# Five instead of six of twelve multiplications by C on GpSimd, in the scan of a hybrid vision kernel

## The chip, the cores and the metric

The kernel runs on one core of one Trainium2 chip. A core has TensorE (PE, matrix products; its weight loads are listed apart as PEld), VectorE (DVE), ScalarE (ACT), GpSimd (POOL) and SyncE (SP, which here issues the DMA transfers). Each engine works through its own instructions in the order in which they were issued to it, and waits for others through semaphores. The metric is the device time of one execution in microseconds; lower is better. Three runs of the kernel before took 6701.09 to 6705.06 us, median 6704.47.

## What is computed

The input is a batch of four images of 96 channels and 64 x 64 pixels. Four layers follow each other; only the first matters here. It normalises the image, expands it to 192 channels, applies a 3 x 3 depthwise convolution and SiLU, and then runs a selective scan over the 4096 pixels in four directions (K = 4: rows, columns, and both reversed), with 16 states for each channel:

```
def step(hst, inp):
    ut, dt_, bt, ct = inp
    dA = jnp.exp(dt_[..., None] * A[None])
    hst = hst * dA + (dt_ * ut)[..., None] * bt[:, :, None, :]
    y = jnp.einsum('bkdn,bkn->bkd', hst, ct)
    return (hst, y)
h0 = jnp.zeros((b, K, DI, N), jnp.float32)
_, ys = jax.lax.scan(step, h0, (u_t, d_t, B_t, C_t))
```

So for each state: a decay exp(delta x A), an input delta x u x B, the recurrence h = h x decay + input, the product h x C, and a sum of these products over the 16 states. The other layers are an inverted residual convolution block, a Fourier attention with a feed-forward block in rounded numbers, and a linear attention with such a block.

## The kernel before

**Tiling of the scan.** A step is one image, one direction and one chunk of 512 pixels: 4 x 4 x 8 = 128 steps. The 192 x 16 states of a step are cut into 12 units (`PC`, numbered u = 0 to 11), each of two halves (e = 0, 1) of 128 partitions by 512 pixels, where the 128 partitions are 32 channels by 4 states. That makes 1536 units. The order of the units within a step is two channel blocks for each of four groups of states (u = 0 to 7), then the third channel block for the four groups (u = 8 to 11).

**What a unit does.**
- `inputs` (L1206): GpSimd multiplies delta x u by B for both halves at once (128 x 1024), into `db`, which has three buffers.
- `decays` (L1216): ScalarE takes two exponentials into two PSUM banks `ps_da`. Four banks have that tag, so two units are there at a time.
- `states` (L1225): VectorE runs the recurrence, one instruction for each half. Its start value comes from the state that the unit of the same number left in the step before.
- The product with C, on one of two engines. In a GpSimd unit the scan writes to an SBUF tile `hc` (five buffers), and `product` (L1244) multiplies both halves in place with one GpSimd instruction. In a VectorE unit the scan writes back over its own PSUM bank, and VectorE multiplies each half right behind its scan from there into `hc` (L1229).
- `keep`: the last column of the states is put by for the next step: by two small copies on ScalarE in a VectorE unit (L1239), by one on GpSimd in a GpSimd unit (L1241). In the last chunk of a direction nothing is kept.
- `sums` (L1265): TensorE adds up over the states, four matmuls for each unit into a bank `ps_y`, for pairs of units (0 and 1, 2 and 3, and so on). At the end of each pass ScalarE takes the bank out (L1276), and SyncE stores it.

Which engine multiplies is fixed by one list, `POOL_C` at L45, read where the units are made (L1169, `"pool": u in POOL_C`). The functions that ask for it are these:

```
x["h"] = [x["hc"][:, e] for e in (0, 1)] if x["pool"] else x["da"]
...
                if not x["pool"]:
                    x["made"] = nc.vector.tensor_mul(x["hc"][:, e], x["h"][e], x["step"]["BC"][x["j"]][:, 1])
...
                if not x["pool"]:
                    nc.scalar.copy(to[:, e : e + 1], x["h"][e][:, end : end + 1])
                elif e == 0:
                    nc.gpsimd.tensor_copy(to, x["hc"][:, :, end])
```

**The order on the engines.** The scan is written under a manual schedule: the order of the program is the order on each engine. A turn of the loop (a slot) deals with one unit and its neighbours: transfers due for the next step and stores (SyncE); `keep` for unit slot - 1 and `decays` for unit slot + 1; `product` for unit slot - 1, if it is a GpSimd unit; `inputs` for unit slot + 2; `states` for unit slot; and the sums of a pair two turns after its second unit.

**The work beside the scan.** The convolutions, norms and the other layers of the neighbouring images fill the same engines. They are written as generators in stages ("front", "turn", "conv", "spectral", "layer_2", "layer_3"). At the end of each turn, `advance` takes steps from them as long as a budget of work for this turn (`owed`, `rate`) and a room for each engine (`room`, `SHARE`) allow it, by prices in microseconds that are written beside each step. None of these asks for `POOL_C`. Operations that appear in the text are, in the front stage, the three ScalarE steps of softplus (L603 to L607), VectorE's L609 and L612 behind them, and ScalarE's copy L616, which gives the bank back; and VectorE's L872 in the layer norms. After the last unit, from about 6210 us, the rest of the last image runs alone.

Of the kernel before, what the change touches and what calls it, by code (L numbers as in the profile page):

```python
# [41 lines left out]
KORDER = [(0, 1, 3, 2)] * (B - 1) + [(1, 3, 0, 2)]  # L42

SCAN = {"rep_d": 3, "rep_g": 3, "rep_BC": 5, "db": 3, "hc": 5}
POOL_C = (1, 3, 5, 7, 9, 11)  # L45
TMP, IN = 10, 5

PC = NI * NJ // 2
# [46 lines left out]
def hybrid_kernel(ctx: ExitStack, tc: tile.TileContext, a: dict):  # L95
# [1052 lines left out]
    def scans(stages):  # L1148
# [13 lines left out]
        for number, step in enumerate(steps):  # L1162
            step["at"] = number % (K * NCH)
            u = 0
            for which, chans in enumerate(PASSES):
                for j in range(NJ):
                    for i in chans:
                        units.append({"step": step, "number": number, "u": u, "j": j, "i": i, "pass": which,
                                      "pool": u in POOL_C})  # L1169
                        u += 1  # L1170
# [402 lines left out]
```

## Time and profile before

| | us |
|---|---|
| median of three runs | 6704.47 |
| the profiled execution | 6709.47 |
| span of its instructions | 6707.7 |
| VectorE busy, 60 to 6210 us | 5304.58 |
| GpSimd busy, 60 to 6210 us | 5480.56 |
| ScalarE busy, 60 to 6210 us | 3990.90 |
| TensorE busy, 60 to 6210 us | 4405.08 |

The profile is of one execution. A row of its costliest groups has the line, the engine, the operation, output and inputs by name, their shapes and the number of instructions; then the busy time in us and the mean in ns; then the idle time of the engine just before these instructions with what ended most of it. Busy time counts each moment of an engine once, so that overlapping instructions add up to less than number times mean. A line of busy time in a stretch gives the stretch, its length, the busy time of each engine with the number of instructions, the granted clock of TensorE (1 is full), the share of the DMA engines and GB/s. A line of waits gives the waiting engine, its output and line, what it waited for, then the sum in us, how often, and the longest. The scan runs from about 70 to 6210 us of the span. GpSimd has almost nothing but the scan: L1206, L1244 and L1241.

### The profile page before, as it was taken

The numbers are of one execution on the slowest core, as the hardware profiler recorded it, in microseconds if no ns is written. First come the engines' busy times: TensorE is split into PE (matmuls) and PEld (weight loads), VectorE is DVE, ScalarE is ACT, GpSimd is POOL, SyncE is SP. The second block draws the span as 40 slices with busy tenths as digits, with TensorE's granted clock in tenths as the row PEclk, the third lists the DMA queues.
The fourth block names the chain that finished last, engine by engine and source line by source line (L and its number), as shares of the span: only waits on it lengthen the run. The fifth ranks groups of instructions, "written<-read, shape, count | busy, mean of one in ns | idle before, by whom it ended". The sixth has DMA issues, their size and how long they took to land. (4 is left out here: it accounts for less than half of the span.)

```text
span 6707.7 us, 84354 instructions
## 1 busy us (share of the span) xinstructions
PE 4872.1 (73%) x27884; PEld 1775.4 (26%) x27884; DVE 5391.2 (80%) x5611; ACT 4269.2 (64%) x8008; POOL 5488.7 (82%) x2983
## 2 busy tenths in 40 slices
PE   7624767656987776775688877777887776859998
PEld 2101212111223521221122254211223521212383
DVE  5979888788989888888899887988988888888021
ACT  5744776654665677877466657866665676756356
POOL 4868778788999999977999988999999899899000
PEclk9756878768998887886799877878998877869998
DMA  5644555566544544455764445465644554554131
GB/s 189 197 150 144 183 189 181 174 218 219 184 148 143 199 158 147 155 186 188 246 214 146 143 160 167 157 219 186 188 147 146 189 161 161 200 180 156 35 94 38
DMA packets 438824, 1121.41 MB, mean 167 GB/s; under 512 B 73002, under 2 KB 74768, under 8 KB 437140
## 3 DMA queue, kind: packets, MB, share of 16 engines
q1 hardware_dynamic: 438388, 1116.02, 50.7%
q8 instruction: 222, 3.64, 0.2%
q14 instruction: 214, 1.75, 0.1%
HBM read 881.28 MB, written 239.01 MB: 167 GB/s over the span
## 5 line engine op out<-in xcount | busy, mean ns | idle before, releaser
L1206 POOL TENSOR_TENSOR db<-rep_g,rep_BC 128x1024 f32<-128x1024 f32 x1536 | 3602.0, 2365 | 194.1 <-DVE ps_da L1225 115.0
L1216 ACT ACTIVATE ps_da<-rep_d,aneg 128x512 f32<-128x512 f32 x3072 | 2053.5, 689 | 499.4 <-DVE hc L1225 381.7
L1225 DVE TENSOR_TENSOR_SCAN ps_da<-ps_da,state,db 128x512 f32<-128x512 f32 x1344 | 1722.9, 1282 | 371.8 <-ACT state L1239 226.7
L1244 POOL TENSOR_TENSOR hc<-hc,rep_BC 128x1024 f32<-128x1024 f32 x768 | 1813.4, 2361 | 131.8 <-DVE hc L1225 64.8
L1225 DVE TENSOR_TENSOR_SCAN hc<-ps_da,state,db 128x512 f32<-128x512 f32 x1344 | 1645.8, 1266 | 173.0 <-ACT ps_da L1216 155.9
L1265 PE MATMUL ps_y<-hc,cst 128*32 128x512 f32 x6144 | 1037.4, 755 | 781.5 <-POOL hc L1244 759.5
L1229 DVE TENSOR_TENSOR hc<-ps_da,rep_BC 128x512 f32<-128x512 f32 x1536 | 1062.3, 692 | 91.3 <-DVE ps_da L1225 1.3
L1265 PEld LDWEIGHTS ps_y<-hc,cst 128*32 128x32 f32 x6144 | 141.7, 119 | 1450.8 <-POOL hc L1244 1096.0
L1241 POOL COPY state<-hc 128x2 f32<-128x2 f32 x672 | 128.4, 191 | 395.3 <-DVE hc L1225 374.1
L1239 ACT COPY state<-ps_da 128x1 f32<-128x1 f32 x1344 | 212.8, 158 | 343.9 <-DVE hc L1229 343.0
L805 PE MATMUL ps_mm<-h,wd 128*32 128x512 f32 x3192 | 365.7, 593 | 7.7 <-ACT r L154 7.0
L543 PE MATMUL ps_mm<-xp,taps 128*128 128x512 f32 x576 | 299.3, 660 | 42.5 <-ACT xp L523 15.7
L1276 ACT COPY yt<-ps_y 128x512 f32<-128x512 f32 x256 | 149.9, 585 | 222.3 <-PE ps_y L1265 212.2
L594 PE MATMUL ps_mm<-xd,dtw 128*128 128x512 f32 x256 | 176.9, 785 | 156.9 <-ACT z L616 131.9
L782 PE MATMUL ps_mm<-wd,w 128*32 128x512 f32 x2128 | 271.4, 624 | 22.9 <-DMA wd<-x 12.8
L1225 DVE TENSOR_TENSOR_SCAN ps_da<-ps_da,db 128x512 f32<-128x512 f32 x192 | 234.6, 1222 | 56.9 <-ACT state L1239 36.0
L1225 DVE TENSOR_TENSOR_SCAN hc<-ps_da,db 128x512 f32<-128x512 f32 x192 | 223.4, 1204 | 17.3 <-ACT ps_da L1216 13.2
L603 ACT ACTIVATE z<-ps_mm 128x512 f32<-128x512 f32 x192 | 114.3, 596 | 189.1 <-PE ps_mm L594 112.4
L609 DVE SCALAR_TENSOR_TENSOR ps_mm<-ps_mm,z 128x512 f32<-128x512 f32 x192 | 131.9, 687 | 84.0 <-ACT z L607 56.4
L864 PE MATMUL ps_mm<-r,cst 128*128 128x512 f32 x210 | 144.9, 778 | 62.7 <-ACT r L154 17.4
L940 PE MATMUL ps_mm<-wa,xp 128*64 128x96 f32 x1728 | 133.3, 317 | 71.0 <-DVE d L944 62.3
L786 ACT ACTIVATE h<-ps_mm 128x512 f32<-128x512 f32 x266 | 153.9, 596 | 44.6 <-PE ps_mm L782 42.5
(418 smaller groups left out, 6879.9 us busy)
## 6 DMA issues: line engine op xcount, KB each, us to landing
rep_BC<-bc SPq DMA_DIRECT2D x512, 512.0 KB
rep_g<-du SPq DMA_DIRECT2D x384, 512.0 KB
rep_d<-delta SPq DMA_DIRECT2D x384, 512.0 KB
y<-yt SPq DMA_DIRECT2D x512, 128.0 KB
du<-g SPq DMA_DIRECT2D x128, 256.0 KB
delta<-z SPq DMA_DIRECT2D x128, 256.0 KB
tab<-in_etab SPq DMA_DIRECT2D x128, 256.0 KB
ypart<-y SPq DMA_DIRECT2D x72, 256.0 KB
```

The costliest lines, as they stand in the source:

```text
L543: mm(p, lhsT=taps[:, t, 0:128], rhs=window(t, c + e), start=t == 0, stop=t == 8)
L594: mm(p, lhsT=dtw[:, o + 2 * part, 0:128], rhs=xd, start=True, stop=True)
L782: mm(p[32 * n : 32 * n + 32], lhsT=w1[:, 32 * g : 32 * g + 32], rhs=xin[:, n : n + 15 : 2, 1 : W + 1], start=True, stop=True)
L786: act(h[:, :, 1 : W + 1], split(p), AF.Relu)
L805: mm(p[32 * n : 32 * n + 32], lhsT=held["wd"][:, groups[i], o, dx, :], rhs=here[i][:, :, dx : dx + W], start=dx == 0, stop=dx == 2)
L1206: nc.gpsimd.tensor_mul(x["db"], x["step"]["g"][x["i"]], both(x["step"]["BC"][x["j"]][:, 0]))
L1216: act(x["da"][e], x["step"]["d"][x["i"]][:, e], AF.Exp, scale=aneg[:, av : av + 1])
L1225: nc.vector.tensor_tensor_scan(x["h"][e][:, order], x["da"][e][:, order], x["db"][:, e, order], start, ALU.mult, ALU.add)
L1229: x["made"] = nc.vector.tensor_mul(x["hc"][:, e], x["h"][e], x["step"]["BC"][x["j"]][:, 1])
L1239: nc.scalar.copy(to[:, e : e + 1], x["h"][e][:, end : end + 1])
L1244: x["made"] = nc.gpsimd.tensor_mul(x["hc"], x["hc"], both(x["step"]["BC"][x["j"]][:, 1]))
L1265: done = mm(y[32 * q : 32 * q + 32], lhsT=const("stack"), rhs=x["hc"][:, e], start=first or (x["pass"] == 0 and x["j"] == 0), stop=last or ...
```

## The change

One list is changed. In each step GpSimd multiplies by C in units 1, 3, 6, 8 and 10 instead of 1, 3, 5, 7, 9 and 11; units 0, 2, 4, 5, 7, 9 and 11 are VectorE units, where 0, 2, 4, 6, 8 and 10 were.

```diff
@@ -42,7 +42,7 @@
 SCAN = {"rep_d": 3, "rep_g": 3, "rep_BC": 5, "db": 3, "hc": 5}
-POOL_C = (1, 3, 5, 7, 9, 11)
+POOL_C = (1, 3, 6, 8, 10)
 TMP, IN = 10, 5
```

Over the 128 steps, 128 units go from GpSimd to VectorE. With a unit goes the place of its states (PSUM bank instead of `hc`) and the engine of its state copies.

## The prediction

> **What bounds the kernel now.** I read the busy shares of the page first, then the costliest groups, then busy time in stretches of the span, then the waits inside three of those stretches. The chain of waits I left aside: it begins at 6139 us, near the end of the scan, so it says nothing of the loop that is changed.
>
> ```profile
> PE 4872.1 (73%) x27884; PEld 1775.4 (26%) x27884; DVE 5391.2 (80%) x5611; ACT 4269.2 (64%) x8008; POOL 5488.7 (82%) x2983
> ...
> L1206 POOL TENSOR_TENSOR db<-rep_g,rep_BC 128x1024 f32<-128x1024 f32 x1536 | 3602.0, 2365 | 194.1 <-DVE ps_da L1225 115.0
> ...
> L1225 DVE TENSOR_TENSOR_SCAN ps_da<-ps_da,state,db 128x512 f32<-128x512 f32 x1344 | 1722.9, 1282 | 371.8 <-ACT state L1239 226.7
> L1244 POOL TENSOR_TENSOR hc<-hc,rep_BC 128x1024 f32<-128x1024 f32 x768 | 1813.4, 2361 | 131.8 <-DVE hc L1225 64.8
> L1225 DVE TENSOR_TENSOR_SCAN hc<-ps_da,state,db 128x512 f32<-128x512 f32 x1344 | 1645.8, 1266 | 173.0 <-ACT ps_da L1216 155.9
> ...
> L1229 DVE TENSOR_TENSOR hc<-ps_da,rep_BC 128x512 f32<-128x512 f32 x1536 | 1062.3, 692 | 91.3 <-DVE ps_da L1225 1.3
> ...
> L1241 POOL COPY state<-hc 128x2 f32<-128x2 f32 x672 | 128.4, 191 | 395.3 <-DVE hc L1225 374.1
> L1239 ACT COPY state<-ps_da 128x1 f32<-128x1 f32 x1344 | 212.8, 158 | 343.9 <-DVE hc L1229 343.0
> ```
>
> GpSimd (POOL) and VectorE (DVE) stand within two points of each other. The 1536 products for `db` are 12 units in each of 128 steps; the 768 products for `hc` are the six units that the change reduces. The other six are 1536 half-width products at L1229 on DVE. The last two rows are the state copies, two for a DVE unit on ScalarE (ACT), one for a GpSimd unit.
>
> The average hides three kinds of stretch:
>
> ```profile
> core 0: us, PE busy (x) PEld busy (x) DVE busy (x) ACT busy (x) POOL busy (x), PEclk, DMA share, GB/s
> 1660.00:2110.00 450.00, 379.34 (x2244) 107.31 (x2246) 408.88 (x416) 285.63 (x556) 444.98 (x244) 0.93 0.50 163
> 460.00:610.00 150.00, 35.61 (x148) 7.39 (x140) 147.38 (x163) 55.16 (x109) 115.26 (x57) 0.50 0.45 152
> 660.00:1410.00 750.00, 516.30 (x1526) 143.97 (x1522) 623.63 (x657) 525.10 (x968) 571.16 (x311) 0.79 0.56 181
> ```
>
> The first is POOL at 98.9%, the second DVE at 98.3%, in the third neither is full (DVE 83%, POOL 76%, ACT 70%). In the first, the waits of DVE in that window name its master, and POOL waits for no engine:
>
> ```profile
> DVE ps_da L1225 <- POOL db L1206: 29.3, 42, 1.1
> DVE ps_da L1225 <- ACT state L1239: 2.5, 3, 1.2
> ```
>
> In the third, ACT waits for a cool TensorE (granted clock 0.79), and DVE for ACT:
>
> ```profile
> ACT z L603 <- PE ps_mm L594: 62.7, 36, 5.1
> ACT z L603 <- PE ps_mm L598: 40.6, 26, 3.1
> ACT ub L556 <- PE ps_mm L552: 34.5, 8, 7.9
> ```
>
> I cut the scan from 60 to 6210 us into 123 slices of 50 us and took, for each, the busy time of each engine and of the `db` products; busy time of those products over 2.345 us (3602.0/1536) is the number of units, a twelfth of it the number of steps. With DVE at 47.5 us or more I call a slice DVE-bound, else with POOL at 47 or more POOL-bound:
> - POOL-bound: 58 slices, 66.8 steps of 43.4 us; mean DVE 44.6, POOL 49.1.
> - DVE-bound: 15 slices, 14.6 steps of 51.3 us; mean DVE 48.7, POOL 42.2.
> - neither: 50 slices, 46.6 steps of 53.6 us (DVE about 39.7, POOL about 40.0).
>
> **What the Trainium skill says.** "Trainium Kernel Development and Optimization", Key Constraints: GpSimd has no access to PSUM. That fits the two forms of L1225: a GpSimd unit scans into `hc`, a DVE unit into the PSUM bank `ps_da`. "GPSIMD Engine Reference", 3 Performance versus the Vector engine: a two-input elementwise operation is about twice as fast on VectorE. Here one unit costs 2361 ns on POOL and 2 x 692 = 1384 ns on DVE, a ratio of 1.7. The same page, 1 Specifications: both engines share SBUF interfaces, and DVE instructions with two SBUF inputs contend. L1229 reads one operand from PSUM, so more of it shouldn't slow POOL; the trace agrees so far as L1206 has a median of 2362 ns with L1229 running beside it. "Perfetto Trace Analysis", Identifying Performance Opportunities: the most contended engine can change between regimes, which is what the slices show.
>
> **The change part by part, for one step of 12 units.**
> - POOL loses one `hc` product, 2361 ns, and in 7 steps of 8 one state copy, 191 ns: 2361 + 167 = 2.53 us, 324 us over 128 steps.
> - DVE gains two products of 692 ns, and two scans that write PSUM instead of SBUF (1282 for 1266 in the rows, medians 1281 and 1260, so 2 x 0.021): 1.43 us, 183 us in all.
> - ACT gains two copies of 158 ns in 7 of 8 steps: 0.28 us, 35 us in all. Each is issued ahead of an exponential in ACT's order. Bounds: 0 where ACT waits for DVE anyway (343 us before L1239), 0.28 where it is the last to come.
> - The positions move from every odd unit to 1, 3, 6, 8, 10. DVE units now stand side by side at 4, 5 and at 11, 0. A DVE unit takes 2 x (1282 + 692) = 3.95 us, a GpSimd unit 2 x 1.27 = 2.53 us of DVE. POOL has 4.9 us of work where it follows a GpSimd unit and 2.35 elsewhere. Two DVE units in a row (7.9 us) against POOL's 7.2 or so for the same pair of turns let POOL run up to 1.6 us ahead; it can't go further than `db`'s three buffers. I looked for a loop that alternates between the engines and is longer than either alone: going from POOL to DVE leads to the unit two places on (a `db` is made for the unit after next), so each such alternation skips a unit of at least 2.35 us, and the most that it can pick up at a DVE pair is 3.95 - 2.35 = 1.6 us. So no mixed loop is longer, and the new order costs nothing as long as ACT is in time. Bounds: 0 to 0.7 us a step (one DVE product of a pair unhidden).
> - TensorE's sums: the same 4 matmuls a unit. For pair 4, 5 they no longer wait for POOL, and the GpSimd products of 6, 8, 10 come a turn earlier than those of 7, 9, 11 did. PE's 759.5 us of waiting before L1265 falls; I take nothing for it, since what it sets free is ACT's background, late only in the third kind of stretch (gain there 0 to 0.3 us a step).
> - No DMA, and no place of the background work in the queues, depends on the list: a turn of the loop is filled by fixed prices. SP's order is unchanged.
>
> **The sum by kind of stretch.**
> POOL-bound: in each slice I add 1.43 us a step to DVE, take 2.53 from POOL, keep the larger and divide by 0.989, the share that POOL itself reaches now. The 58 slices come to 2754 us instead of 2900: -146. The two loads have become almost equal (sums 2713 and 2708), so what is late next is DVE. In ten of the slices TensorE is 46 us busy or more of 50; holding each slice to its TensorE time gives 2767, -133. I take three quarters of this, since DVE isn't as even as POOL: its background comes in bunches and it has ACT upstream. -100 us, 1.5 us a step. Ends: -133 and -30.
> DVE-bound: 14.6 x 1.43 = +21 us; DVE's added work is bare here.
> Neither: DVE's 1.43 and ACT's 0.28 are 1.71 us a step, were all of it on the path. In the third window DVE idles 17% and it is ACT and TensorE that it waits for, but ACT's last copy of a front block (L616) in turn stands behind DVE's L609, which queues behind the scans. I take half, 0.85 x 46.6 = +40 us. Ends: 0 and +80.
> Sum: -100 + 21 + 40 = -39 us. The profiled execution took 6709.47 us (span 6707.7), 5.0 over the median of the runs, 6704.47. So 6670.5 for a run like the profiled one, and against the median 6665.
>
> **The rivals.**
> - The full gain (0.09): POOL-bound slices reach -133, and the DVE time added in the third kind hides behind ACT and TensorE (+15). -133 + 21 + 15 = -97: 6607. For: POOL waits on no engine in the first window. Against: DVE's bursts.
> - A draw (0.11): only half of -133 comes, and in the third kind a little over half of the 80 is paid: -66 + 21 + 45 = 0, so 6704.
> - Slower (0.36): DVE becomes the engine that everything queues behind. Place: DVE's in-order queue at L1225/L1229, with L609, L872 and the other background operations behind it; they give banks back to TensorE and inputs to ACT. Price: all of 1.71 us in 61.2 steps outside the POOL-bound slices, +105, and behind the pairs of DVE units ACT's exponentials come late, so that the POOL-bound steps keep only 0.5 us: -33. Sum +72: 6776. It decides from the point where the POOL-bound steps gain less than what the others pay: (21 + 40)/66.8 = 0.9 us a step with half the price, 1.6 with the whole. For: DVE waits 262.7 us for L1239 and 169 us for L1216 already. Against: in the POOL-bound window only 2.5 us of those.
> - That the change doesn't do what it says I give nothing: the flag alone chooses the branch in states, keep and product.
>
> **How the numbers follow.** Forecast 6665 with chance 0.44, its own range 6635 to 6690. Full gain 0.09, draw 0.11, slower 0.36. The range takes in the full gain and the lower half of the slower case: 6600 to 6760. This kernel's runs lie within 4 us of each other, so 0.2%, 13 us, is about what can be told from no change. Faster 0.53, within 0.2% 0.11, slower 0.36.
>
> **What would show it.** L1244 x640 at about 2360 ns, L1229 x1792 at 692, L1239 x1568, L1241 x560. From 1660 on the same work in about 432 us instead of 450, DVE near 98% and POOL near 95, and POOL waiting for DVE (L1225) where it waited for nothing. In 460 to 610 a stretch longer by about 4 us. DVE's busy time about 5574, POOL's about 5165. Wrong would be: DVE well under 95% in the conv stretches with waits for ACT, which would mean that the new order of units costs more than its work; or the front stretches (660 to 1410) longer by more than 23 us, that is the whole 1.71 us in each of its 13.3 steps (160 units).

## The result, and the profile after

The changed kernel takes 6710.65 us, median of 20 runs, against 6704.77 for the kernel before in 20 runs beside it. The ratio is 1.0011, 95% interval 1.0004 to 1.0018: slower by about a tenth of a per cent, inside the 0.2% that the prediction counted as no change. The forecast was 6665. The 20 runs of the kernel before spread over 22 us (6692.90 to 6715.30), where the prediction, from three, took 4.

The page of the changed kernel, busy shares and the groups that answer to those shown of before:

```profile
PE 4846.8 (72%) x27884; PEld 1770.8 (26%) x27884; DVE 5551.4 (83%) x5867; ACT 4312.1 (64%) x8232; POOL 5178.2 (77%) x2743
...
L1206 POOL TENSOR_TENSOR db<-rep_g,rep_BC 128x1024 f32<-128x1024 f32 x1536 | 3599.2, 2362 | 508.3 <-DVE ps_da L1225 412.6
...
L1225 DVE TENSOR_TENSOR_SCAN ps_da<-ps_da,state,db 128x512 f32<-128x512 f32 x1568 | 2006.6, 1280 | 280.4 <-ACT state L1239 216.1
L1244 POOL TENSOR_TENSOR hc<-hc,rep_BC 128x1024 f32<-128x1024 f32 x640 | 1509.7, 2359 | 136.7 <-DVE hc L1225 77.2
...
L1229 DVE TENSOR_TENSOR hc<-ps_da,rep_BC 128x512 f32<-128x512 f32 x1792 | 1239.3, 692 | 113.6 <-PE ps_y L1265 3.8
L1239 ACT COPY state<-ps_da 128x1 f32<-128x1 f32 x1568 | 247.7, 158 | 459.4 <-DVE hc L1229 456.0
...
L1241 POOL COPY state<-hc 128x2 f32<-128x2 f32 x560 | 105.0, 187 | 388.5 <-DVE hc L1225 358.5
```

The work moved as the diff says, to the instruction: 640 products on GpSimd at 2359 ns, 1792 on VectorE at 692 ns. GpSimd is busy 310 us less (5488.7 to 5178.2), VectorE 160 more. But GpSimd's idle time before L1206 rose from 194 to 508 us: what it was spared, it waits for VectorE's scans. With 256 more VectorE products in the run, the products of the two engines took as long as before (2362, 2359 and 692 ns), so the contention between them that the prediction looked for doesn't show.

The same three stretches of the span, after:

```profile
core 0: us, PE busy (x) PEld busy (x) DVE busy (x) ACT busy (x) POOL busy (x), PEclk, DMA share, GB/s
1660.00:2110.00 450.00, 388.95 (x2264) 111.39 (x2264) 437.08 (x454) 300.58 (x603) 438.92 (x236) 0.94 0.54 175
460.00:610.00 150.00, 33.88 (x138) 7.12 (x138) 147.31 (x155) 52.52 (x103) 101.23 (x50) 0.50 0.44 145
660.00:1410.00 750.00, 519.36 (x1553) 146.26 (x1552) 636.18 (x677) 522.36 (x982) 538.26 (x288) 0.80 0.55 179
```

In the first, the conv stretch, VectorE now reaches 97.1% and GpSimd still 97.5%: the two meet, as the sum expected. VectorE's waits in that window are almost gone; of the 29.3 us for GpSimd's `db` none is left (the view lists gaps of more than 0.15 us):

```profile
DVE ps_da L1225 <- ACT state L1239: 1.8, 3, 1.1
DVE ps_da L1225 <- ACT ps_da L1216: 0.8, 1, 0.8
DVE ps_mm L735 <- PE ps_mm L733: 0.8, 1, 0.8
```

So this stretch got faster, and something else was lost. To find it, both traces were cut at the first recurrence instruction of each of the 128 steps. Steps were put into classes by their busy shares before: GpSimd at 97% or more (57 steps: 37 in the conv stages and the last image's scan, 20 elsewhere), else VectorE at 95% or more (14), else mixed (57). Summed over the steps of each class, in us against the trace of before, with the experiments below beside it:

| class before | steps | the change | e1 | e2 | e10 | e6 | e13 |
|---|---|---|---|---|---|---|---|
| GpSimd full, conv | 37 | -48.1 | -68.5 | -0.5 | -62.8 | -50.4 | -2.6 |
| GpSimd full, elsewhere | 20 | +20.5 | +8.4 | +9.5 | +12.3 | +1.9 | +23.2 |
| VectorE full | 14 | +22.7 | -6.3 | +17.5 | +22.3 | -0.9 | +20.4 |
| mixed | 57 | +12.2 | -30.3 | +9.3 | -4.7 | -4.4 | +14.8 |
| all | 128 | +7.3 | -96.8 | +35.8 | -32.9 | -53.8 | +55.8 |

Each column is one profiled execution, so a few us in a class mean nothing: e5, which changes almost nothing, shows +6.1 in the second row and -6.7 in the fourth. The classes were picked in the trace of before, so steps that were short there by chance tend to come out longer elsewhere; in the 20 steps e6, which leaves them as they were, has +1.9. A few us of every entry in the second row, the change's +20.5 too, are no effect.

### The profile page after: what moved, and what is told of

It reads as the page before. It is cut to its first block, busy times and chain, and to the rows that moved or that the text cites. A ratio compares the mean times of both kernels' runs of the same rounds, so it can differ in the third digit from the quotient of the medians.

```text
span 6713.7 us, 84574 instructions
## 1 busy us (share of the span) xinstructions
PE 4846.8 (72%) x27884; PEld 1770.8 (26%) x27884; DVE 5551.4 (83%) x5867; ACT 4312.1 (64%) x8232; POOL 5178.2 (77%) x2743
## 5 line engine op out<-in xcount | busy, mean ns | idle before, releaser
L1206 POOL TENSOR_TENSOR db<-rep_g,rep_BC 128x1024 f32<-128x1024 f32 x1536 | 3599.2, 2362 | 508.3 <-DVE ps_da L1225 412.6
L1216 ACT ACTIVATE ps_da<-rep_d,aneg 128x512 f32<-128x512 f32 x3072 | 2065.8, 690 | 481.1 <-DVE hc L1225 337.4
L1225 DVE TENSOR_TENSOR_SCAN ps_da<-ps_da,state,db 128x512 f32<-128x512 f32 x1568 | 2006.6, 1280 | 280.4 <-ACT state L1239 216.1
L1244 POOL TENSOR_TENSOR hc<-hc,rep_BC 128x1024 f32<-128x1024 f32 x640 | 1509.7, 2359 | 136.7 <-DVE hc L1225 77.2
L1225 DVE TENSOR_TENSOR_SCAN hc<-ps_da,state,db 128x512 f32<-128x512 f32 x1120 | 1371.3, 1266 | 116.9 <-ACT ps_da L1216 81.2
L1265 PE MATMUL ps_y<-hc,cst 128*32 128x512 f32 x6144 | 1018.4, 741 | 584.3 <-DVE hc L1229 285.7
L1229 DVE TENSOR_TENSOR hc<-ps_da,rep_BC 128x512 f32<-128x512 f32 x1792 | 1239.3, 692 | 113.6 <-PE ps_y L1265 3.8
L1239 ACT COPY state<-ps_da 128x1 f32<-128x1 f32 x1568 | 247.7, 158 | 459.4 <-DVE hc L1229 456.0
L1241 POOL COPY state<-hc 128x2 f32<-128x2 f32 x560 | 105.0, 187 | 388.5 <-DVE hc L1225 358.5
L1225 DVE TENSOR_TENSOR_SCAN ps_da<-ps_da,db 128x512 f32<-128x512 f32 x224 | 273.3, 1220 | 43.7 <-ACT state L1239 40.2
L1225 DVE TENSOR_TENSOR_SCAN hc<-ps_da,db 128x512 f32<-128x512 f32 x160 | 186.1, 1204 | 15.2 <-ACT ps_da L1216 9.0
```

Source lines behind the costliest of these rows:

```text
L1206: nc.gpsimd.tensor_mul(x["db"], x["step"]["g"][x["i"]], both(x["step"]["BC"][x["j"]][:, 0]))
L1216: act(x["da"][e], x["step"]["d"][x["i"]][:, e], AF.Exp, scale=aneg[:, av : av + 1])
L1225: nc.vector.tensor_tensor_scan(x["h"][e][:, order], x["da"][e][:, order], x["db"][:, e, order], start, ALU.mult, ALU.add)
L1244: x["made"] = nc.gpsimd.tensor_mul(x["hc"], x["hc"], both(x["step"]["BC"][x["j"]][:, 1]))
L1265: done = mm(y[32 * q : 32 * q + 32], lhsT=const("stack"), rhs=x["hc"][:, e], start=first or (x["pass"] == 0 and x["j"] == 0), stop=last or ...
```

## The experiments

Times are medians; ratios are against runs of the kernel before on the same chip, with 95% intervals. The kernel before had medians between 6702.23 and 6703.65 there. Three theories were held against each other at first. A, the one of the forecast: a step whose GpSimd is full is paced by GpSimd. B: only the conv stage is; elsewhere a full GpSimd merely fills the time that the others need. C: the order of the units costs the time.

**e1: GpSimd's relief alone.**

```diff
-                if units[slot - 1]["pool"]:
+                if units[slot - 1]["pool"] and units[slot - 1]["u"] != 5:
```

> Six on GpSimd as before, but the product with C of unit 5 is left out in all 128 steps (so that unit reaches the sum without its C): POOL does 128 x 2.36 us less, VectorE nothing more. Theory A (what the prediction used: all steps with GpSimd near full are paced by GpSimd): the 57 steps with GpSimd at 97% or more go from 43.0 to about 40.8 us, -125 us in all, 6580. Theory B (only the conv stage is paced by GpSimd; in the attention and feed-forward stages the full GpSimd only fills the time that VectorE and ScalarE need): the 37 conv steps gain about 2.2 us each, -80, the 20 others nothing, 6625. Theory C (the order of the units costs the time): as A, since the order is kept.

6609.18 us, 0.9856 (0.9842 to 0.987), between A and B. The classes decide: conv -68.5, and the 20 other full steps +8.4 (e5: +6.1), though GpSimd had 2.36 us less to do in each. That is B. The 30 us that the mixed steps gain neither theory had; half of them (14.9) come from the ten mixed steps with GpSimd at 94 to 97%. A stretch outside conv shows B in one view: busy time from 2340 to 2780 us, of the kernel before, then of e1, then of the changed kernel.

```profile
2340.00:2780.00 440.00, 294.22 (x1256) 96.01 (x1249) 388.57 (x396) 351.36 (x672) 425.94 (x235) 0.78 0.46 152
```

```profile
2340.00:2780.00 440.00, 293.41 (x1008) 82.53 (x1007) 387.22 (x394) 347.95 (x673) 401.85 (x223) 0.77 0.46 150
```

```profile
2340.00:2780.00 440.00, 295.55 (x1397) 102.41 (x1394) 395.33 (x412) 351.96 (x679) 397.92 (x213) 0.79 0.46 153
```

The fifth busy time is GpSimd's: 96.8% before, 91.3% in e1. VectorE's, the third, stays at 388 and 387: as much of its work was done in the same 440 us, so the pace didn't follow GpSimd. In the kernel before this window is steps 44 to 53. Cut by steps, these ten took 440.9 us before, 447.4 in e1, and 447.4 in e5 and 443.8 in e6, whose products there are those of before: 23.6 us less of GpSimd work bought nothing. Whom VectorE waited for there was to be read before the change too; its longest waits in that window, kernel before:

```profile
DVE ps_da L1225 <- ACT state L1239: 19.4, 20, 2.4
DVE hc L1225 <- ACT ps_da L1216: 8.2, 11, 1.5
DVE ps_da L1225 <- POOL db L1206: 7.0, 10, 0.9
```

ScalarE 27.6 us, GpSimd 7.0. In e1 the same two lines for ScalarE stand at 23.0 and 10.1 us. In the conv stretch it had been GpSimd 29.3 and ScalarE 2.5. GpSimd is nearly as full here (96.8%) as there (98.9%); the releaser of VectorE's waits is another.

**e2: VectorE's load alone.**

```diff
                     x["made"] = nc.vector.tensor_mul(x["hc"][:, e], x["h"][e], x["step"]["BC"][x["j"]][:, 1])
+                elif u == 5:
+                    nc.vector.tensor_mul(x["da"][e], x["da"][e], x["step"]["BC"][x["j"]][:, 1])
```

> Six on GpSimd as before, and two extra VectorE products of 128 x 512 behind the scans of unit 5, in place in their PSUM banks, which nothing reads: VectorE does 128 x 1.4 us more, GpSimd nothing less. Theory A: +20 us in the 14 steps that VectorE bounds, up to +40 in the 57 mixed ones, 0 in the 57 full ones: about 6750. Theory B: the same +20, +10 to +20 in the mixed ones, 0 in the conv steps and +1 us in each of the 20 full steps outside conv: about 6755, told from A by those 20 steps. Theory C: as A.

6742.46 us, 1.0054 (1.004 to 1.0068). In conv the added work is free (-0.5, GpSimd covers it), in the steps that VectorE fills it is bare (+17.5), in the mixed ones it costs a ninth of the forecast's price for all of it (9.3 of 57 x 1.43 = 82). The 20 steps have +9.5, half of what B said. So in those 20 neither engine's work alone sets the pace; what does, no run singles out. The two halves add up to -53 us, but the change has +6. They can't simply add in conv, since each alone is measured beside an engine that has slack; e16 below measures how little that is, 11 us.

**e3 and e4: the same amounts in other orders.** e3 is five on GpSimd, 1, 3, 5, 7, 9; e4 is six, 2, 3, 5, 8, 9, 11.

```diff
-POOL_C = (1, 3, 5, 7, 9, 11)
+POOL_C = (1, 3, 5, 7, 9)
```

> Five on GpSimd, units 1, 3, 5, 7, 9: the same amounts as the change, but three VectorE units in a row (10, 11, 0). Theories A and B (amounts decide): within 10 us of the changed kernel, 6700 to 6720. Theory C (runs of VectorE units cost time, because ScalarE's exponentials or POOL's db come out of step): slower than the changed kernel by 20 us or more, 6730 and over.

> Six on GpSimd in another order, units 2, 3, 5, 8, 9, 11: the amounts of the kernel before, with two pairs of VectorE units and two of GpSimd units side by side. Theories A and B: within 10 us of the kernel before. Theory C: slower by 20 us or more, with waits for ACT before the scans.

e3: 6713.22 us, 1.0016 (1.0009 to 1.0023), like the changed kernel, against C. e4: 6757.49 us, 1.0076 (1.0062 to 1.009), against A and B: with six, order can cost 55 us. e4 has two GpSimd units side by side, which no five of this study has.

**e9 and e10: the change's amounts, spread evenly in the old order.**

```diff
+                elif e == 1:
+                    nc.vector.tensor_mul(x["da"][1][:, :66], x["da"][1][:, :66], x["step"]["BC"][x["j"]][:, 1, :66])
...
-            x["made"] = nc.gpsimd.tensor_mul(x["hc"], x["hc"], both(x["step"]["BC"][x["j"]][:, 1]))
+            n = CH - 99
+            x["made"] = nc.gpsimd.tensor_mul(x["hc"][:, :, :n], x["hc"][:, :, :n], x["step"]["BC"][x["j"]][:, 1:2, :n].to_broadcast([128, 2, n]))
```

> Units and order as before (six on GpSimd at 1, 3, 5, 7, 9, 11), but the change's amounts of work spread evenly: each GpSimd product covers 2 x 426 of 2 x 512 columns (the last 86 of each half go to the sum without C), about 0.39 us less, and each such unit has one extra VectorE product of 128 x 172 in place in its PSUM bank, about 0.25 us, which nothing reads. No state copy moves. If the amounts alone decide (GpSimd's relief and VectorE's load meet in each step, the order is free): like the change, 6700 to 6715. If the order of the units or the copies cost the rest: the sum of the two halves measured before, -93 + 40 = -53, so about 6650.

> As e9_spread, with the widths set by what it measured (346 ns for 172 columns, 692 for 512, so about 240 for 66; GpSimd 2.1 ns a column): VectorE gets 6 products of 128 x 66 a step, about 1.43 us, GpSimd's products cover 2 x 413 columns, about 2.5 us a step less; 99 columns of each half go to the sum without C. These are the change's amounts in the order of before. If the order of the units costs what is missing: 6650 to 6670. If the amounts meeting in each step do: 6695 to 6715.

e9 (widths 172 and 86) took 6706.9 us, 1.0009 (1.0001 to 1.0017), but missed its aim: a VectorE product of 172 columns took 346 ns and not 250, 2.07 us a step in place of 1.43. e10 (the widths above: 234 ns, 1.40 us a step) has the change's amounts: 6672.05 us, 0.995 (0.9938 to 0.9963). The amounts alone make the kernel faster by 31 us. The 38 us up to the changed kernel come with what else the list changes. The pieces and the shortened GpSimd products, e9 first, then e10:

```profile
L1247 POOL TENSOR_TENSOR hc<-hc,rep_BC 128x852 f32<-128x852 f32 x768 | 1533.1, 1996 | 128.5 <-DVE hc L1225 95.2
...
L1231 DVE TENSOR_TENSOR ps_da<-ps_da,rep_BC 128x172 f32<-128x172 f32 x768 | 265.5, 346 | 26.6
```

```profile
L1247 POOL TENSOR_TENSOR hc<-hc,rep_BC 128x826 f32<-128x826 f32 x768 | 1493.2, 1944 | 126.5 <-DVE hc L1225 98.1
...
L1231 DVE TENSOR_TENSOR ps_da<-ps_da,rep_BC 128x66 f32<-128x66 f32 x768 | 179.9, 234 | 26.6
```

**e5 and e8: copies, and the place in the pair, at six.** e5 makes the two state copies of unit 4 twice; e8 has the list 0, 2, 4, 6, 8, 10.

```diff
                     nc.scalar.copy(to[:, e : e + 1], x["h"][e][:, end : end + 1])
+                    if u == 4:
+                        nc.scalar.copy(to[:, e : e + 1], x["h"][e][:, end : end + 1])
```

> Kernel before with the two state copies of unit 4 made twice on ScalarE: 0.28 us more of ScalarE in 7 of 8 steps, as the change adds, nothing else. If the copies are what the sum of the two halves lacks: +30 us or more. If they lie in ScalarE's waits: 0 to +10 us.

> Six on GpSimd at 0, 2, 4, 6, 8, 10: amounts and alternation of the kernel before, but GpSimd's unit is now the first of each pair of the sums and stands elsewhere against the background work, as in the change's units 6, 8 and 10. If this phase costs time: +20 us or more (the change has it in half of each step). If only neighbours of one kind cost: within 10 us of the kernel before.

e5: 6708.8 us, 1.0012 (1.0003 to 1.002), 5 us, within what was expected of hidden copies. e8: 6743.23 us, 1.0065 (1.0052 to 1.0077): with six, the first place of the pair costs 40 us. It was a suspect for the change, whose units 6, 8 and 10 stand so.

**e14, e15 and e16: the same suspects at the change's balance.** e14 is e10 with e5's copies, e15 is e10 with e8's list, e16 is e1 and e2 in one kernel.

> e10_spread_as_change with the two state copies of unit 4 made twice (0.28 us of ScalarE in 7 of 8 steps, the change's amount); 99 columns of each half of a GpSimd product go to the sum without C, as there. If copies make part of the missing 38 us once VectorE is the bound: 6685 or more. If not: 6672 to 6680, e5's +5.

> e10_spread_as_change with the GpSimd units at 0, 2, 4, 6, 8, 10 (first of each pair of the sums); the same 99 columns go to the sum without C. If the place in the pair costs what it costs at six (e8: +40): about 6710, and the change, which has it in 3 of its 5 GpSimd units, owes it about half of 38. If VectorE's load hides it: 6672 to 6680.

> e1 and e2 in one kernel: unit 5 is a GpSimd unit whose product with C is left out, with two extra VectorE products in its PSUM banks that nothing reads. Amounts as in e10, but all in one unit, so that units 4, 5 and 6 are heavy on VectorE in a row; no copies, no PSUM writes more. If heaping costs: 6685 to 6698 (e11 has 6698). If e11's excess over e10 is copies and PSUM writes: 6672.

e14: 6684.84 us, 0.9971 (0.9959 to 0.9982), 13 us over e10 by the medians and just under the 6685 from which the copies were to count; the intervals of the two just overlap, so the size is rough. e15: 6677.81 us, 0.9959 (0.9946 to 0.9971): the place in the pair, 40 us at six, isn't to be told from nothing here. e16: 6661.93 us, 0.9935 (0.9921 to 0.9948): heaping all of VectorE's added work on one unit, beside two heavy ones, costs nothing either; it is even 10 us below e10, though the intervals overlap. Two of three suspects fell.

**e11: e16 done by the list itself.** Five on GpSimd, 1, 3, 7, 9, 11.

> Five on GpSimd at 1, 3, 7, 9, 11, three VectorE units in a row at 4, 5, 6. It is the two halves measured before put together at the same unit (e1 and e2 both at unit 5), with copies and PSUM writes as in the change. If the halves simply add: 6650. If they don't, as the change and the list 1, 3, 5, 7, 9 say: 6700 to 6720 whatever the list.

6698.16 us, 0.9991 (0.9982 to 0.9999), 36 us over e16, and 12 under the changed kernel with the same amounts. So 36 us (32 in the two traces) belong to what a unit brings along when it really moves. Its groups beside those of e16 (first e16, where L1231 is the extra product and L1241 the copies; then e11):

```profile
L1216 ACT ACTIVATE ps_da<-rep_d,aneg 128x512 f32<-128x512 f32 x3072 | 2057.4, 690 | 542.3 <-DVE hc L1225 287.6
...
L1229 DVE TENSOR_TENSOR hc<-ps_da,rep_BC 128x512 f32<-128x512 f32 x1536 | 1062.5, 692 | 90.6 <-DVE ps_da L1225 0.9
...
L1241 ACT COPY state<-ps_da 128x1 f32<-128x1 f32 x1344 | 212.8, 158 | 361.9 <-DVE hc L1229 359.0
...
L1231 DVE TENSOR_TENSOR ps_da<-ps_da,rep_BC 128x512 f32<-128x512 f32 x256 | 175.8, 687 | 4.4
```

```profile
L1216 ACT ACTIVATE ps_da<-rep_d,aneg 128x512 f32<-128x512 f32 x3072 | 2065.8, 690 | 446.9 <-DVE hc L1225 303.9
...
L1229 DVE TENSOR_TENSOR hc<-ps_da,rep_BC 128x512 f32<-128x512 f32 x1792 | 1239.3, 692 | 108.0 <-DVE ps_da L1225 1.4
...
L1239 ACT COPY state<-ps_da 128x1 f32<-128x1 f32 x1568 | 246.9, 157 | 461.0 <-DVE hc L1229 457.2
```

The 224 copies more are 34 us of ScalarE. They have 98 us more of waiting for VectorE in front of them, but the exponentials (L1216) have 95 us less, so the waiting has mostly moved. e14, whose added copies stand behind others that have waited already, says 13 us of time.

VectorE's own part shows in the two traces: from the start of its first scan to the end of its last product, unit 5 takes 3.77 us in e16 and 3.98 us in e11 (means of 128), 28 us more in all. Most of it lies in when the products start. In e16 the extra product starts on average 24 ns before the recorded end of the scan ahead of it; in e11 the real one starts 101 ns after it in the first half and 35 ns in the second. The groups, which count no gap below zero, show 13 us of this (108.0 against 90.6 + 4.4). The scans are 8 ns longer each, 2 us. That the real product reads what the scan has just written isn't shown to be the reason: the extra products of e9 and e10 don't read it either and start 35 ns after (26.6 us/768).

Copies and VectorE together would be 41 us, more than the 36, so probably not all of it costs time, and how the 36 divide isn't shown. e9 warns against counting VectorE's time in full: it has 86 us more of VectorE's products than e10 and 40 us more of GpSimd's, and is only 35 us slower.

**e6, e13 and e12: the list chosen by stage.**

```diff
-POOL_C = (1, 3, 5, 7, 9, 11)
+POOL_C = {6: (1, 3, 5, 7, 9, 11), 5: (1, 3, 6, 8, 10), 7: (1, 3, 4, 5, 7, 9, 11)}
+FIVE = {*range(29, 39), *range(66, 76), *range(93, 104), *range(120, 124)}
...
-                                      "pool": u in POOL_C})
+                                      "pool": u in POOL_C[5 if number in FIVE else 6]})
```

> The list is chosen by step: five (1, 3, 6, 8, 10) in the 35 steps of the conv stages (29 to 38, 66 to 75, 93 to 103, 120 to 123), six (1, 3, 5, 7, 9, 11) in all others. Where the gain is the conv stage's and the loss the others': -40 to -48 us, about 6660. If the gain in conv is given back by later stages that then come to wait: within 15 us of the kernel before.

> The other half of e6: five (1, 3, 6, 8, 10) in all steps but the 35 of the conv stages, six there. Theory B (outside conv the full GpSimd is no bound, so five costs and gains nothing): +50 to +60, about 6758, so that with e6's -50 it makes the change's +7. Theory A (GpSimd bounds there too): 6700 or less.

> As e6_five_in_conv, and seven on GpSimd (1, 3, 5, 6, 8, 10, 11) in 13 steps that VectorE bounds (4 to 8, 23, 39, 42, 61, 76, 77, 104, 107). If those steps are paced by VectorE alone, each gives 1.43 us back: -18 against e6, about 6635. If GpSimd units side by side cost as they do in e4: 6650 or more.

e6: 6652.79 us, 0.9926 (0.9914 to 0.9939). e13, its complement: 6759.59 us, 1.0081 (1.0068 to 1.0095). -51 and +57 make the change's +6: this is the whole result, taken apart. e12, with seven on GpSimd in thirteen steps (twelve of them in the VectorE-full class), took 6650.32 us, 0.9921 (0.9908 to 0.9935), not to be told from e6 where 18 us less was expected if VectorE alone paces those steps: the VectorE-full class gained 10.6 us in its trace (e6 0.9), the mixed steps lost 4.6 where e6 had won 4.4. The page of e6 has both engines within one point over the whole span:

```profile
PE 4854.7 (73%) x27884; PEld 1772.2 (27%) x27884; DVE 5427.1 (82%) x5681; ACT 4278.8 (64%) x8070; POOL 5404.7 (81%) x2917
```

e6 beats the kernel before and the changed one, by 51 and 58 us.

## Why the prediction was wrong

Two steps of the prediction failed. It took every full GpSimd for the bound, and it put what a moved unit brings along, beyond the work itself, at almost nothing.

**The conv stretches: right.** 33 of the 58 slices that the prediction called POOL-bound lie in the conv stages and the last image's scan, and they hold half of its floor (worked out again from the slices of the trace of before). So about -50 of the -100 was meant for them; the 37 conv steps gave -48 (timed in e6: -51). Steps 29 to 38 took 432.4 us before and 413.4 after. VectorE became the bound, GpSimd stood just behind it, as said.

**The other slices with a full GpSimd: the first step that failed.** It was the sentence that puts every slice with GpSimd at 47 us of 50 into one class "POOL-bound" and takes three quarters of its floor. 20 of 57 steps had the fullness without the bound. They gave +20.5 instead of the other -50, a miss of some 70 us. e1 shows it: with GpSimd alone relieved they gained nothing. The waits of VectorE would have told the two apart; the prediction read them in the conv stretch and carried the reading to the rest.

**VectorE-bound slices: right.** +21 forecast, +22.7 measured.

**The mixed slices: priced too high.** +40 forecast at half of 1.71 us a step, +12 measured; steps 10 to 23, about the window from 660 to 1410 us, went from 787.0 to 795.2 us, where the full price was 23. VectorE's work is mostly hidden there (e2: +9.3; behind whom was not tested), and GpSimd's relief, which the prediction gave nothing here, is worth 30 us alone (e1). The miss of 28 us makes up for part of the 70.

**"So no mixed loop is longer, and the new order costs nothing as long as ACT is in time": the second step that failed.** No cost of the heaping was found (e16), and none clear of noise of the place in the pair at this balance (e15). But a unit that really moves costs 36 us more than its amounts (e11 against e16), and the sum had next to nothing for it. ScalarE's copies are some 13 of them (e14, rough); they were priced at 0.28 us a step, but entered the sum at half, in the mixed slices alone. The later start of VectorE's products was in no term; with it a unit takes 0.22 us longer on VectorE than the same amounts do in e16.

Four measurements lay this out in order: the two halves added give -53 us (e1 and e2), both together -42 (e16), with what a moved unit brings along -5 (e11), and in the change's order +6. The amounts alone give 6672 (e10) or 6662 (e16), near the forecast of 6665, but by luck in part: there two errors cancel, the 20 steps taken too good and the mixed ones too bad. What was left uncancelled, 36 us of companions and 12 of order, made the outcome a draw.

**What stays open.** Lists of five with the same amounts differ: 6698 (1, 3, 7, 9, 11), 6711 (the change), 6713 (1, 3, 5, 7, 9). So do e4 among the sixes, and e8, whose 40 us shrink to 6 once the change's amounts are moved (e15 against e10). The background work has fixed places by turn, and which units meet which of it changes with the list; no run isolates it. Open as well are what paces the 20 steps in place of GpSimd, and how the 36 us divide between ScalarE's copies and VectorE's later products.

**The slower rival** was right that the steps outside conv pay (e13, +57; that VectorE's queue is the place there wasn't tested) but kept only 33 us of gain in the full steps; it was 6776 against 6711. The draw came out, for another reason than it gave.

## What to carry to other kernels

An engine at 97% of a stretch need not be its bound; here it was one only where VectorE waited for it. Read whose release ends the waits of the second busiest engine, stretch by stretch, before giving a full engine's relief its floor. Where stages have different bounds, choose the split of work by stage; one list for all steps gave back in one what it won in the other. When work moves between engines, list what moves along with it (here ScalarE's copies, the memory that results land in, and how early the product can start behind its scan) and price it on the engine that will then be the bound.

## What the runs showed of the hardware

A VectorE product with one input in PSUM took 234 ns for 66 columns (e10) and 346 for 172 (e9), both written to PSUM, and 692 for 512 written to SBUF: about 1.02 ns a column (346/340) over some 170 ns that don't shrink. Cutting work into thin pieces for balance pays that each time: e9's six pieces, 1032 columns, took 2.07 us a step, half as long again as two pieces with 1024 columns (1.38). GpSimd's product took 1944 ns for 826 columns (e10), 1996 for 852 (e9) and 2361 for 1024, about 2.1 ns for each further column.

VectorE's instructions can overlap in the trace. Where two scans of a GpSimd unit follow each other, the second starts 83 ns before the recorded end of the first (median). In e16 the extra product, which overwrites the bank that the scan ahead of it has read, starts 83 ns before that end where the scan runs forward through the pixels, as the product does, and 34 ns after it where the scan runs in reverse.
